# A two-layer attention kernel: residual sums through an identity product, and the seam between the layers cut into pairs of tiles

## The chip, the cores and the metric

The kernel runs on one core of a Trainium2 chip. The core has a matrix engine (TensorE, PE in the profile), a vector engine (VectorE, DVE), a scalar engine (ScalarE, ACT), a general engine (GpSimd, POOL) and SyncE (SP), which here only issues DMAs. The metric is the device time of one execution in microseconds (us); the three timed runs gave 1856.75, 1857.15 and 1862.86, median 1857.15.

## What is computed

Two layers work on x, two sequences (b = 0, 1) of 1024 rows by 512. Cut to the places that matter here:

```
xn = layernorm(x)
x  = x + attention0(xn) + mix(xn)          # layer 0
xn = layernorm(x)
x  = x + attention1(xn) + lora_ffn(xn)     # layer 1, causal, 32 heads, 8 groups

attention0: one head of 128;  out @ Wo + bo
mix:        H_res = (1-g)*I + g*sinkhorn(logits)      # 4x4 per row, 50 iterations
            x_mixed[i] = sum_j H_res[i,j] * xn_stream[j]      # 4 streams of 128
            + a small branch product, spread over the 4 streams
attention1: latent = xn @ Wdown;  k, v = latent @ Wup;  q = xn @ Wq;  out @ Wo
```

## The kernel before

**Tiles and data.** A tile is 128 rows of x; each sequence has eight, t = 0 to 7. `acc[b, t]` (128x512, f32) holds the running residual of a tile through both layers. Every product that must have f32 accuracy is taken in f16: both factors are split into a high and a low part, and three of the four partial products are summed in PSUM (`mm3`, line 83, whose matmul is line 88). There are eight PSUM banks, in three rings: `pp` (four), `s` (three, taken by `srow()`), and `av` (one, `out_tile()`).

**Order.** The program is written out straight, and the scheduler of the language keeps each engine's queue near the written order, filling in instructions that are ready. An engine then runs its own queue in order. Where the order must not be left to the scheduler, the source pins it with `after(...)` or `behind(...)`.

**Layer 0.** For each sequence `front0` normalises and transposes and makes Q, K, V and the logits of the mix. `attn0_rows` (line 457) computes softmax rows, four row blocks per half. `attn0_out` (line 468) multiplies with V, evacuates, splits (lines 476 to 479), and for each of four tiles adds in one PSUM bank the bias (line 484) and the three products with Wo (line 486). VectorE then adds the bank to `acc` (line 488). It is called four times, 16 tiles in all.

**The Sinkhorn chain.** For b = 0 it runs on VectorE (`chain_dve`, line 561): 49 iterations of six small instructions each (lines 576 to 583), every one needing the one before it. It is a generator; `adv(n)` in the main program takes n half iterations of it between other pieces of layer 0, and `adv(200)` (line 997) takes what is left once the attention of b = 1 is written. Line 592 makes the last product, line 527 scales it into `Hm`, and line 529, four times, adds the diagonal. The kernels of the chain lie in one `s` bank.

**The seam.** Layer 1 begins with b = 0. Lines 1011 to 1022 mix, normalise and transpose its tiles in two groups of four (`LG`). Tiles in `MP` (1, 3, 6, 7) are mixed by ScalarE (16 multiplications of 128x128, line 633) and GpSimd (four sums, line 634), the others by VectorE (16 instructions, line 642) from a PSUM copy of `acc` that ScalarE makes (line 614), in an `s` bank for tiles 0 and 2 and in a `pp` bank for tiles 4 and 5. `layernorm_tiles` (line 214) takes the statistics of a group (lines 219, 220), and a short reciprocal square root between VectorE and ScalarE (lines 221 to 224, 201, 202). `normed_T` (line 227) scales (lines 233, 237), splits (238, 240) and issues a transposing DMA per tile (line 242) into `xT`. `after` holds VectorE's j > 0 mixing of group 1 behind group 0's norm (line 224) and ScalarE's j > 1 mixing behind group 0's last split.

**Layer 1's first products.** `start` (line 1024) makes four latent blocks from tiles 0 to 3, the four query blocks of half 0 from the same tiles, four latent blocks from tiles 4 to 7, and then the first keys and values. Each block is 12 matmuls of 512 columns. A latent block is evacuated by four ScalarE and four VectorE instructions of 64x256 (`lat_evac`, line 663). After that the attention of layer 1 goes on to the end of the kernel.

## Time and profile before

| stage of the profiled execution (us from its start) | what happens |
|---|---|
| 0 to 180.5 | layer 0, its Sinkhorn chain interleaved |
| 180.5 to 197.5 | rest of the chain on VectorE, last products of layer 0 |
| 197.5 to 225.2 | mix, norm and transposition of tiles 0 to 3; no matmul |
| 225.2 to 259.7 | layer 1's first products; tiles 4 to 7 follow |
| 261.9 to 1853.7 | attention of layer 1 |

The profiled execution took 1855.46 us, its span from first to last instruction is 1853.7 us, so 1.8 us lie around the span. PE is busy for 93% of the span, DVE 78%, ACT 64%, POOL 49%. In the lines that follow further down, a timeline row reads: start, duration (of one or of a merged run), engine, line, operation, output<-input, shapes, count, and in brackets the idle time before it with what ended that idle time. A row of windows gives, for one stretch, its length and the busy time and count of PE, PEld (weight loads), DVE, ACT and POOL, then the granted TensorE clock, the DMA share and GB/s. A row of waits gives who waited for whom, the sum in us, how often, and the longest.

### The profile page before, as it was taken

To read this page: it belongs to the slowest core of one execution; us is meant where nothing else is said; L and a number is where in the kernel's file an instruction comes from. 1 tells how busy PE (TensorE), PEld (TensorE's weight loads), DVE (VectorE), ACT (ScalarE), POOL (GpSimd) and SP (SyncE) were. 2 spreads that over 40 slices of the span, in tenths; PEclk is the share of its full clock that TensorE was granted. 3 is DMA by queue.
4 is the path that set the end of the run, shared out by engine and by line. 5 is a ranking of instruction groups with operands and counts; after the bars stand their busy time and mean duration, and the time that the engine had idled before them with its cause. 6 is when DMAs were issued, how large, how long until landed. Compare 5 with 4: busy or idle time off the path is not lost. (4 is left out here: it accounts for less than half of the span.)

```text
span 1853.7 us, 35094 instructions
## 1 busy us (share of the span) xinstructions
PE 1715.7 (93%) x11458; PEld 1046.0 (56%) x11458; DVE 1447.6 (78%) x4050; ACT 1194.1 (64%) x2917; POOL 910.6 (49%) x1540
## 2 busy tenths in 40 slices
PE   4756399999999999998999999999999999999998
PEld 3434146566666556655555556666666666656565
DVE  8888978988888877777976867777777777777675
ACT  3848665656676778776544756666666767676554
POOL 5567639768775455647634333424242433335200
PEclk9878699999999999999999999999999999999999
DMA  7435225666574657468546555656565656566455
GB/s 211 82 56 124 67 51 131 143 115 144 113 147 102 143 115 158 111 131 158 137 92 141 130 120 126 146 111 150 107 151 115 142 117 140 117 141 139 101 123 120
DMA packets 707306, 230.26 MB, mean 124 GB/s; under 512 B 689953, under 2 KB 690081, under 8 KB 707122
## 3 DMA queue, kind: packets, MB, share of 16 engines
q1 hardware_dynamic: 691666, 180.75, 47.2%
q0 software_dynamic: 13152, 43.07, 8.5%
q10 hardware_dynamic: 2304, 4.20, 0.7%
q8 instruction: 90, 1.47, 0.4%
q14 instruction: 94, 0.77, 0.1%
HBM read 52.81 MB, written 4.19 MB: 31 GB/s over the span
## 5 line engine op out<-in xcount | busy, mean ns | idle before, releaser
L291 ACT ACTIVATE P<-P,nm 128x1024 f32<-128x1024 f32 (+31 forms) x528 | 391.3, 742 | 250.0 <-DVE nm L283 234.8
L314 DVE SCALAR_TENSOR_TENSOR Phl<-P,r,Phl 128x1024 f16<-128x1024 f32 (+31 forms) x515 | 434.4, 853 | 85.9 <-ACT Phl L308 79.5
L88 PE MATMUL s<-K,Q 128*128 128x512 f16 (+22 forms) x2400 | 440.7, 317 | 19.5 <-DVE P L287 11.6
L345 PE MATMUL av<-PT,V 128*128 128x256 f16 x3648 | 447.7, 274 | 7.5 <-DMA PT<-Phl 6.8
L345 PEld LDWEIGHTS <-V 128*128 128x128 f16 x3648 | 357.0, 98 | 94.7 <-DMA PT<-Phl 8.3
L308 ACT ACTIVATE Phl<-P,r 128x1024 f16<-128x1024 f32 (+31 forms) x515 | 370.0, 731 | 22.3 <-DMA PT<-Phl 3.3
L88 PE MATMUL pp<-xT,wq 128*128 128x512 f16 x1536 | 372.9, 381 | 6.3 <-DVE acc L737 3.2
L88 PE MATMUL pp<-wo,ao 128*128 128x512 f16 x1536 | 369.9, 379 | 2.9 <-ACT ao L104 2.7
L94 POOL TENSOR_SCALAR f2k<-f2k 128x512 f32<-128x512 f32 x164 | 109.5, 668 | 499.9 <-DVE Phl L314 444.5
L88 PEld LDWEIGHTS <-Q 128*128 128x128 f16 x2400 | 223.2, 98 | 178.2 <-issue 28.4
L88 PEld LDWEIGHTS <-wq 128*128 128x128 f16 x1536 | 149.6, 98 | 173.8 <-issue 8.5
L88 PEld LDWEIGHTS <-ao 128*128 128x128 f16 x1536 | 149.4, 98 | 156.5 <-ACT ao L104 4.8
L287 DVE TENSOR_SCALAR_CACHE_REDUCE P<-s 128x512 f32<-128x512 f32 (+15 forms) x272 | 152.6, 562 | 21.7 <-PE s L88 19.7
L283 DVE CUSTOM_DVE_ANT_0 P<-s,mask,nm 128x272 f32<-128x272 f32 (+15 forms) x256 | 157.3, 615 | 8.7 <-PE s L88 1.0
L303 ACT ACTIVATE r<-r 128x1 f32<-128x1 f32 x528 | 96.2, 193 | 66.2 <-DVE r L302 65.4
L319 POOL MEMSET Phl<- 128x192 f16 (+2 forms) x384 | 72.6, 209 | 133.5 <-DMA PT<-Phl 95.7
L302 DVE RECIPROCAL r<-r 128x1 f32<-128x1 f32 x528 | 79.2, 155 | 75.3 <-ACT P L291 72.1
L104 ACT ACTIVATE ao<-av 128x512 f16<-128x512 f32 x128 | 75.1, 587 | 92.2 <-PE av L345 92.0
L283 DVE CUSTOM_DVE_ANT_0 P<-s,mask 128x32 f32<-128x32 f32 (+15 forms) x256 | 104.3, 432 | 27.6 <-PE s L88 27.1
L104 ACT ACTIVATE Q<-pp 128x512 f16<-128x512 f32 x128 | 74.5, 582 | 76.7 <-PE pp L88 72.2
L737 DVE SCALAR_TENSOR_TENSOR acc<-pp,acc 128x512 f32<-128x512 f32 x128 | 87.4, 682 | 41.0 <-PE pp L88 40.6
L105 DVE SCALAR_TENSOR_TENSOR Q<-pp,Q 128x512 f16<-128x512 f32 x128 | 87.6, 684 | 34.9 <-ACT Q L104 34.6
(254 smaller groups left out, 2119.1 us busy)
## 6 DMA issues: line engine op xcount, KB each, us to landing
f2k<-in_Wq POOLq DMA_DIRECT2D x64, 256.0 KB, 3.2
f2k<-in_WoT POOLq DMA_DIRECT2D x64, 256.0 KB, 3.3
PT<-Phl SPq DMA_TRANSPOSE x528, 3.2
acc<-in_x SPq DMA_DIRECT2D x16, 256.0 KB, 4.6
f2k<-in_Wup POOLq DMA_DIRECT2D x16, 256.0 KB, 3.5
out<-acc ACTq DMA_DIRECT2D x16, 256.0 KB, 3.5
xr<-in_x SPq DMA_DIRECT2D x12, 256.0 KB, 4.1
f2k<-in_Wlat POOLq DMA_DIRECT2D x8, 256.0 KB, 5.5
```

What stands on the lines that cost most here:

```text
L88: nc.tensor.matmul(dst, lhs(l), rhs(r), start=(i == 0 and j == 0), stop=(i == n - 1 and j == 2))
L94: first = G.tensor_scalar(stage, stage, scale, 1.0, ALU.mult, ALU.mult)
L104: A.activation(hl_hi, src, AF.Copy, scale=scale)
L105: return V.scalar_tensor_tensor(hl_lo, src, scale, hl_hi, ALU.mult, ALU.subtract)
L283: last_row[0] = V.tensor_tensor_reduce(Pm[:, o:o + w], pt[:, :w], mask[:, 512 - w:], -scale, first, ALU.add, ALU.min, nm[:, k:k + 1])
L287: last_row[0] = V.tensor_scalar(Pm[:, o:o + w], pt[:, :w], -scale, first, ALU.mult, ALU.min, accum_out=nm[:, k:k + 1])
L291: A.activation(Pm[:, :W], Pm[:, :W], AF.Exp, bias=last, scale=-1.0, accum_out=r[:, 0:1])
L303: A.activation(r[:, 1:2], r[:, 1:2], AF.Copy, scale=PSCALE)
L308: A.activation(hl[:, 0, :W], Pm[:, :W], AF.Copy, scale=r[:, 1:2])
L314: lo = V.scalar_tensor_tensor(hl[:, 1, :W], Pm[:, :W], r[:, 1:2], hl[:, 0, :W], ALU.mult, ALU.subtract)
L345: nc.tensor.matmul(p, Vh(j, l), PT(r * nj + j), start=(j == 0 and k == 0), stop=(j == nj - 1 and k == 2))
L737: V.scalar_tensor_tensor(acc[b, t], p, 1.0 / 256.0, acc[b, t], ALU.mult, ALU.add)
```

## The change

1. In `attn0_out` an identity matrix `eye` of f32 (value 1024, made by GpSimd at the start) times `acc` is summed into the PSUM bank by TensorE. ScalarE then writes the bank, scaled by 1/1024, to `acc`. VectorE's sum at line 488 is gone. For b = 1, half 1, three banks are kept; their writes, and the whole fourth product, are put behind the first pair's last split.
2. The last product of the chain writes `Hm` directly in the wanted order, the scaling is in place, and the four diagonal sums become one with a stride of five.
3. The seam goes in four pairs of tiles; `MP` is (1, 3, 5, 7), so each pair has one tile for VectorE and one for ScalarE and GpSimd. The PSUM copies of tiles 0, 2, 4 and 6 all lie in `s` banks. The pinning of the order is by pairs, and there is none between the third and fourth.
4. `start` takes four latent blocks and two query blocks by quarters of 256 columns: first all six for the first pair, then all six for the second. Query blocks 2 and 3 are whole. The latent blocks of tiles 4 to 7 go by quarters again. Keys and values alternate by half.

```diff
-LG = ((0, 1, 2, 3), (4, 5, 6, 7))
-MP = (1, 3, 6, 7)
+LG = ((0, 1), (2, 3), (4, 5), (6, 7))
+MP = (1, 3, 5, 7)
...
+    eye = T("tw", [P, P], bufs=1)
+    G.memset(eye, 1024.0)
+    G.affine_select(eye, eye, [[-1, P]], ALU.is_equal, 0.0, base=0, channel_multiplier=1)
...
+    def proj_quarter(p, w, xT, k):
+        mm3(p[:, 256 * (k % 2):256 * (k % 2) + 256],
+            [(lambda l, c=c: w(c, l), lambda r, c=c: xT[:, 2 * k:2 * k + 2, 2 * c + r, :])
+             for c in range(NC)])
...
             for r in range(2):
                 nc.tensor.matmul(p, row, bo[:, r], start=(r == 0), stop=False)
+            nc.tensor.matmul(p, eye, acc[b, 4 * half + q], start=False, stop=False)
             for k, (l, r) in enumerate(PASSES):
...
-            V.scalar_tensor_tensor(acc[b, t], p, 1.0 / 1024.0, acc[b, t], ALU.mult, ALU.add)
+        def store(q, p):
+            A.activation(acc[b, 4 * half + q], p, AF.Copy, scale=1.0 / 1024.0)
+        if later is None:
+            for q in range(4):
+                store(q, product(q))
+            return
+        ps3 = [product(q) for q in range(3)]
+        later += [lambda q=q: store(q, ps3[q]) for q in range(3)] + [lambda: store(3, product(3))]
...
-        V.tensor_scalar(Hb, M if b else M.rearrange("p t j i -> p t i j"), gs[:, 0:1], None, ALU.mult)
-        for n in range(4):
-            V.tensor_scalar(Hb[:, :, n, n], Hb[:, :, n, n], gs[:, 1:2], None, ALU.add)
+        V.tensor_scalar(Hb, Hb, gs[:, 0:1], None, ALU.mult)
+        diag = Hb.rearrange("p t i j -> p t (i j)")[:, :, 0::5]
+        V.tensor_scalar(diag, diag, gs[:, 1:2], None, ALU.add)
...
-                    got["d"] = srow() if t < 4 else PP()
+                    got["d"] = srow()
...
-                with after(*(last_rs[:1] if pool else last_rs[1:] if j else last_mix)):
+                with after(*(last_rs[:1] if pool else (last_rs[1:] or last_mix) if j else last_mix)):
...
-        last_rs[:] = [last_hi[0], stt]
+        last_rs[:] = [last_hi[0], stt] if k < 2 else []
+        if k == 0:
+            with after(last_hi[0]):
+                for f in sums:
+                    f()
...
-        for mc in range(4):
-            lat_evac(0, mc, 0, lat_block(0, wl[:, mc], 0))
-        for u in range(4):
-            q(u)
-        for mc in range(4):
-            lat_evac(0, mc, 1, lat_block(0, wl[:, mc], 1))
-        for f in kvf:
-            f()
+        def quarters(todo, th):
+            for k in range(2):
+                for w, p, evacuate in todo:
+                    proj_quarter(p, w, xT1[0], 2 * th + k)
+                    if k:
+                        evacuate(p)
+        quarters(lats(0) + [q_first(u, srow()) for u in range(2)], 0)
+        q(2)
+        q(3)
+        quarters(lats(1), 1)
+        for k in (0, 2, 1, 3):
+            kvf[k]()
```

`lats(th)` puts three latent blocks in `pp` banks and the fourth in the `av` bank; `q_first` evacuates a query block from an `s` bank as `qproj` did.

More of the change, by code (lines that the diff above doesn't have):

```diff
@@ L466, in attn0_rows, with attn0_out @@
         return PTs
-    def attn0_out(b, half, Vh, PTs):
+    def attn0_out(b, half, Vh, PTs, later=None):
         p = out_tile()
@@ L479, in attn0_out, with product @@
         G.tensor_tensor(hl[:, 1], ao, hl[:, 0], ALU.subtract)
-        for q in range(4):
-            t = 4 * half + q
+        def product(q):
             p = PP()
@@ L487, in attn0_out @@
                                  start=False, stop=(k == 2))
-            V.scalar_tensor_tensor(acc[b, t], p, 1.0 / 1024.0, acc[b, t], ALU.mult, ALU.add)
+            return p
+        def store(q, p):
[6 more added lines that the diff above has]
+        later += [lambda q=q: store(q, ps3[q]) for q in range(3)] + [lambda: store(3, product(3))]
     def sinkhorn(b, lg):
@@ L558, in chain_pool @@
                 x = Kt
-        V.tensor_tensor(M, M, over_i(bb), ALU.mult)
+        V.tensor_tensor(Hm[b], M, over_i(bb), ALU.mult)
     def chain_dve(b, Z, M, aa, bb, over_i, over_j, f2):
@@ L591, in chain_dve @@
             yield
-        V.tensor_tensor(f2(M), f2(M), over_j(bb), ALU.mult)
+        V.tensor_tensor(Hm[b].rearrange("p t i j -> p t j i"), M, bc(bb, 3, 4), ALU.mult)
     xr_more, last_mix, last_stt, last_rs = {}, [], [None], []
@@ L728, in qproj, with q_evac @@
     def qproj(b, w, Q, hh, half):
-        p = proj_T(lambda c, l: w[:, l, c, :], xT1[b], half)
+        q_evac(Q, hh, proj_T(lambda c, l: w[:, l, c, :], xT1[b], half))
+    def q_evac(Q, hh, p):
         evac(p.rearrange("p (b q) -> p b q", q=QR), Q[:, 0, :, hh, :], Q[:, 1, :, hh, :], 0.125)
@@ L799, in layer1_attn, with q_first @@
         kvs[0], fs = kv0
-        start(fs[2:], lambda u: q_unit(0, u))
+        def q_first(u, p):
+            if u == 0:
+                Qs[0, 0] = T("Q", [P, 2, NS // 2, 4, QR], F16, bufs=2)
+            return lambda c, l: qw[0, u][:, l, c, :], p, lambda p: q_evac(Qs[0, 0], u, p)
+        start(fs[2:], q_first, lambda u: q_unit(0, u))
         for hh in range(4):
@@ L995, in tile_model @@
         PTs = attn0_rows(1, half, *f0[1][:2], lambda: adv(CD))
-        attn0_out(1, half, f0[1][2], PTs)
+        sums = []
+        attn0_out(1, half, f0[1][2], PTs, sums if half else None)
     adv(200)
@@ L1021, in tile_model, with start, lats @@
             xT_tile(0, t, NP[t])
-        last_rs[:] = [last_hi[0], stt]
-    def start(kvf, q):
-        latents(0)
-        for mc in range(4):
-            lat_evac(0, mc, 0, lat_block(0, wl[:, mc], 0))
-        for u in range(4):
-            q(u)
-        for mc in range(4):
-            lat_evac(0, mc, 1, lat_block(0, wl[:, mc], 1))
-        for f in kvf:
-            f()
+        last_rs[:] = [last_hi[0], stt] if k < 2 else []
[3 more added lines that the diff above has]
+                    f()
+    def start(kvf, q_first, q):
+        latents(0)
+        lat = lambda mc: lambda c, l: wl[:, mc, l, c, :]
+        def lats(th):
+            return [(lat(mc), out_tile() if mc == 3 else PP(), lambda p, mc=mc: lat_evac(0, mc, th, p))
+                    for mc in range(4)]
+        def quarters(todo, th):
[10 more added lines that the diff above has]
+            kvf[k]()
     gw1 = gating_w()
```

## The prediction

> **What bounds the kernel now.** I first asked for busy time by stretches of the span, with the borders set where the seam between the layers begins and ends (the columns are explained above).
>
> ```profile
> 180.50:197.50 17.00, 12.34 (x77) 6.96 (x76) 14.46 (x45) 6.04 (x10) 9.08 (x11) 0.99 0.51 141
> 197.50:225.20 27.70, 0.02 (x1) 0.05 (x2) 26.85 (x88) 22.20 (x71) 20.89 (x18) 0.51 0.22 42
> 225.20:244.30 19.10, 17.51 (x73) 7.32 (x74) 15.30 (x37) 10.67 (x25) 16.18 (x23) 0.91 0.49 112
> 244.30:261.80 17.50, 16.87 (x79) 7.55 (x77) 7.97 (x17) 7.67 (x18) 0.00 (x0) 1.00 0.07 27
> ```
>
> From 197.5 to 225.2 no matmul runs, and VectorE is busy for 26.85 of 27.70 us: there DVE is the bound. From 225.2 on PE is the bound, and stays so: the same view by larger stretches has PE busy for 300.00 of 300 us twice between 1100 and 1700. So what arrives earlier at PE's first product of layer 1, and isn't lost again before the first scores, comes off the end one for one. Next I read the waits of PE, and the timelines of PE (first fence) and DVE (second).
>
> ```profile
> PE pp L88 <- DMA xT<-wo: 29.6, 1, 29.6
> ...
> 225.18 9.57 PE L88 MATMUL pp<-xT,PT 128*128 128x512 f16 x36 [29.63 <-DMA xT<-wo]
> 236.34 2.76 PE L88 MATMUL pp<-xT,PT 128*128 128x512 f16 x12 [1.59 <-DVE cmp L105]
> 238.98 10.53 PE L88 MATMUL pp<-xT,wq 128*128 128x512 f16 x48
> 249.35 10.52 PE L88 MATMUL pp<-xT,PT 128*128 128x512 f16 x48
> 259.71 1.46 PE L88 MATMUL pp<-cmp,wo 128*128 128x512 f16 x6
> 261.86 0.31 PE L88 MATMUL s<-K,Q 128*128 128x32 f16 x4 [0.69 <-ACT K L104]
> ```
>
> PE waits once, 29.6 us, for the transposes of tiles 0 to 3. Then it works with one gap of 1.59 us to the first keys at 259.71. Tiles 4 to 7 don't hold it: their last transpose is issued at about 241, lands 3.2 us later, and the blocks that read it start at 249.35.
>
> ```profile
> 192.46 0.29 DVE L581 TENSOR_TENSOR sk<-s,sk 128x128 f32<-128x128 f32 x1
> 193.46 0.69 DVE L488 SCALAR_TENSOR_TENSOR acc<-pp,acc 128x512 f32<-128x512 f32 x1 [0.71 <-PE pp L486]
> 194.07 0.28 DVE L582 TENSOR_REDUCE sk<-sk 128x32 f32<-128x128 f32 x1
> 194.26 1.28 DVE L488 SCALAR_TENSOR_TENSOR acc<-pp,acc 128x512 f32<-128x512 f32 x2
> 195.46 0.34 DVE L583 RECIPROCAL sk<-sk 128x32 f32<-128x32 f32 x1
> 195.72 0.63 DVE L488 SCALAR_TENSOR_TENSOR acc<-pp,acc 128x512 f32<-128x512 f32 x1
> 196.26 0.28 DVE L592 TENSOR_TENSOR sk<-sk,sk 128x128 f32<-128x128 f32 x1
> 196.57 0.33 DVE L527 TENSOR_SCALAR Hm<-sk,gs 128x128 f32<-128x128 f32 x1
> 196.94 0.64 DVE L529 TENSOR_SCALAR Hm<-Hm,gs 128x8 f32<-128x8 f32 x4
> 197.48 6.29 DVE L642 SCALAR_TENSOR_TENSOR s<-xr,Hm,s 128x128 f32<-128x128 f32 x24
> ```
>
> The end of the Sinkhorn chain is a bare sequence on DVE, and line 488 stands in its way: its sums are queued between the chain's steps, and one waits 0.71 us for PE with the chain behind it.
>
> **Part 1, the sum leaves DVE.** After the last softmax row (180.5) eight sums of line 488 lie in the chain, four from 185.53 to 188.33 and four from 193.46 to 196.26. By start times, from each to the chain's next instruction, they hold DVE for 1.21 + 0.60 + 0.54 + 0.61 + 1.20 + 0.54 = 4.7 us, and two waits for PE of 0.96 and 0.71 us go with them: 6.4 us off. The eight sums of b = 0 (90.9 to 106.1) I cost at nothing: the chain follows its written places (91 of its about 100 steps are placed before the last `adv`), and DVE then idles 2.74 us at 117.6 for a product of b = 1, whose path goes through POOL, busy without a break from 100.8 to 124.4. If the chain did use that time, up to 4.7 + 1.3 = 6 us more would go.
>
> In place of each sum come a ScalarE write and an f32 matmul. The write's nearest row is the copy at line 614 (0.58 to 0.60 us, 128x512 between PSUM and SBUF). ACT is busy for only 6.04 of 17.00 us around 190 and has idle stretches of 11.4 and 10.2 us near 90 and 105; without that cover 16 writes would cost 9.6 us. No f32 matmul is in this trace. Below, it is one f16 matmul, 0.216 us (48 starts in 10.37 us). Above, it is all four partial products of two split factors on a cold array: six f16 matmuls at 85.6 took 2.74, so 4 x 0.46 = 1.83 us. I take 0.8 us, the nearest row: the three-pass product at line 486 (0.82). The Trainium skill, "FP8 and Floating Point Precision", section "TensorE Precision Notes", says that true f32 takes four passes through the array; that would be an estimated 0.86 us and change nothing below. Cover: before each group PE idles for ACT's split (4.96, 0.91, 3.84 and 0.60 us) with `acc` and `eye` ready, so the identity products of the first three tiles go there; the fourth, waiting for a bank, adds 0.8 us. POOL reaches the sums that need them at 108 to 113, after line 488 was done at 106.1, so 0.8 us is hidden. Uncovered, all 16 would be 13 us, at worst 29. The last group's fourth product runs in PE's idle stretch. `eye` is two POOL instructions at about 2 us (rows there: 0.52 for 128x512, 0.24 for a 32x32 selection); if the selection grows with its rows and columns it is 4 us at most, beside POOL's 3.57 us wait for the first weights, so nothing to 1 us.
>
> **Part 2, the chain's end.** Four diagonal sums (0.54 us from first start to the next instruction) become one (0.2): 0.3 us off; the strided product may give 0.1 back. Together with part 1 the mix starts at 197.5 - 6.4 - 0.3 = 190.8, call it E.
>
> **Part 3, pairs.** DVE's tile costs 16 instructions at 0.262 (24 in 6.29) = 4.2 us. ACT's tile is 16 at 0.295 (32 in 9.45) = 4.7, and POOL's last sum 1.3 after it. ACT also has lines 476 and 478 (1.3 us) near 190. So tile 1 is mixed at E + 7.5 where four tiles took until 208.9. Statistics and the short chain: 0.7 + 0.2 + 0.2, 0.6 on ACT with its hand-overs, six DVE instructions 1.5 (229.09 to 230.56): E + 11. Scaling 0.8, two splits 0.6 each, two remainders 0.65 each, overlapped: the second transpose is issued at about E + 14, and with 3.2 us to landing and its 1.25 us of issue PE can start at E + 18 = 209. Before, it was 197.5 + 27.7. The last writes (1.8 us of ACT) follow.
>
> Each further pair repeats this, but with its j = 0, 1 products done while the norm of the pair before runs. What is queued behind the new waits: on DVE 12 mix instructions (3.1), two remainders (1.3) and a scaling (0.5); then POOL's last sum, statistics 0.7, norm 2.5, scaling and splits 2.5, transposes 4.5. I count 10 to 11 us per pair: landings at E + 18, 29, 39. The fourth competes with evacuations of the first latent blocks (16 x 0.42 = 6.7 us of DVE) and lands at about E + 47. DVE's whole work up to there (mix 17, statistics 7, norms 6, scaling and remainders 6.5, evacuations 8) is 44.5 us, which agrees.
>
> **Part 4, quarters.** A matmul of 256 columns takes 0.109 us (24 of line 345 in 2.78 with a last drain of 0.16), so halves cost 12 x (2 x 0.109 - 0.216) = 0.02 us a block more: nothing. Sequence: pair 1, six quarters, 72 x 0.109 = 7.9 and a cold start of 1.7, E + 18 to 27.6; wait to 29; pair 2, 7.9, to 37; query blocks 2 and 3, 5.2, to 42; pair 3, 5.2, to 47.5; pair 4, 5.2, to 52.7 or, with the hand-over, 53. First keys at E + 53 = 244 where they were at 259.7. Gain 15.7 us. The keys' order adds nothing: they need only latent blocks 0 and 1. The `s` banks can bite: query block 1 needs the bank of tile 4, free at about E + 26, when PE gets there at E + 26; a stall of some 1 us is likely. I take 15 us.
>
> The trace on restarts: from 225.2 to 228.6 PE did 9 matmuls at a granted clock of 0.51, then 18 in the next 3.4 us at 1.00, so a cold start costs 1.7 us. The Trainium skill, "TensorE: Matmul & The Clock Gate", section "Part 1: The HAM clock gate", says the array falls back to half rate after an idle window of about 3.4 us. That speaks against work in bursts: by it each gap of that length between pairs would cost a further 1.7, an estimated 5 us for three; with the gaps counted above, none.
>
> **The sum.** 1855.46 - 15 = 1840.5 on the profiled execution, which lies 1.7 us under the median, so 1842.2 against 1857.15. Its own range: 6 us more from b = 0 and a few from earlier landings, 1832; 6 us less from pairs that come late, 1848.
>
> **Rivals.** *The last pair is late.* If nothing of a norm is hidden, a pair takes 12.5 us: landings at E + 18, 30.5, 43, 55.5, keys at E + 60.7, a gain of 8: 1849. For it: DVE is full already (26.85 of 27.70). Against: the work is the same and the last landing before was 46.8 after the chain's end. *The chain doesn't end earlier*, because the scheduler puts something else in the freed places or the f32 products hold b = 1 back: E stays at 197.5, pairs alone give 15 - 6.7 = 8: 1849. *Slower*: the f32 products are long and lie on PE in front of layer 0's products with V. At 1.83 us and all exposed, 29 us against a gain of 15: 1871. It decides from 25 us, that is 1.55 us on each of 16. For it: the clock is 0.64 to 0.93 in those stretches. Against: PE idles 3.8 and 5.0 us in front of two of the groups.
>
> **Chances.** Forecast 0.62; last pair late 0.15; chain not earlier 0.10; slower 0.13. 0.5%, about what a measurement tells from no change, is 9.3 us: faster means under 1847.9. The forecast and a few of the middle cases give 0.65; within 0.5%, 0.21; slower 0.14. The range takes in the middle cases: 1832 to 1853.
>
> **What would show it.** In the profile after: no DVE sum in the chain, the first mix instruction at about 191; first matmul of layer 1 near 209, first keys near 244, with gaps between the quarters under 2 us; the f32 products near 0.8 us in PE's old idle stretches. Wrong if the mix starts at 197 or later, if PE waits more than 5 us in sum between the quarters, if layer 0's products with V move back, or if the attention of layer 1 loses what the seam gained.

## The result, and the profile after

The change is slower: 1874.51 us median of four runs (1871.76 to 1875.19) against 1857.12 for the kernel before (1856.75 to 1862.86), ratio 1.0084 [1.0065, 1.0103]. The forecast was 1842.2, with a range of 1832 to 1853. The profiled execution took 1874.25 us, with a span of 1872.5.

Busy time by stretches of the kernel after, with the columns of the first fence of the prediction. It starts at the same time, 180.5, and the other borders lie at the same events (start of the mix, first product, the middle of the products, first scores):

```profile
180.50:195.50 15.00, 11.02 (x25) 3.41 (x24) 10.92 (x33) 7.40 (x14) 11.64 (x12) 0.61 1.01 240
195.50:221.90 26.40, 16.74 (x67) 7.38 (x66) 12.45 (x37) 14.51 (x37) 6.57 (x6) 0.69 0.18 41
221.90:256.00 34.10, 23.67 (x163) 17.20 (x163) 31.92 (x91) 24.58 (x72) 24.50 (x27) 0.85 0.27 64
256.00:276.60 20.60, 16.03 (x133) 12.12 (x132) 11.84 (x30) 10.02 (x25) 6.29 (x10) 0.95 0.22 52
```

In the second row DVE, full before (26.85 of 27.70), is busy for 12.45 of 26.40 us: it waits. And from the first product to the first scores PE is busy for 39.70 of 54.70 us, where it was 34.38 of 36.60. PE's timeline shows the gaps:

```profile
221.93 3.83 PE L88 MATMUL pp<-xT,PT 128*128 128x256 f16 x24
...
237.21 6.02 PE L88 MATMUL pp<-xT,PT 128*128 128x256 f16 x36 [6.21 <-DMA xT<-wo]
...
248.82 2.76 PE L88 MATMUL pp<-xT,wq 128*128 128x512 f16 x12 [1.66 <-DVE cmp L105]
254.14 4.45 PE L88 MATMUL pp<-xT,wq 128*128 128x512 f16 x12 [2.56 <-DVE cmp L105]
...
266.87 4.10 PE L88 MATMUL pp<-xT,PT 128*128 128x256 f16 x36 [3.03 <-DMA xT<-wo]
...
273.60 0.38 PE L88 MATMUL pp<-cmp,wo 128*128 128x512 f16 x1 [1.32 <-ACT cmp L104]
...
276.61 0.32 PE L88 MATMUL s<-K,Q 128*128 128x32 f16 x4
```

The first product comes 3.3 us earlier than before (221.93 against 225.18), the first keys 13.9 later (273.60 against 259.71). Two gaps of PE wait for transposes, two for evacuations of the latent blocks (`cmp`). The second kind was in the prediction's own fence already: `236.34 ... [1.59 <-DVE cmp L105]`, the fourth latent block waiting for the first one's evacuation. I read it as a small stall; it is the sign that the blocks run out of banks. Here the section on the kernel is wrong: line 46 gives the ring `s` four banks and `pp` three, not the other way round.

DVE's timeline of the kernel after, at the end of the chain and behind the first mix:

```profile
186.56 1.77 DVE L323 SCALAR_TENSOR_TENSOR Phl<-P,r,Phl 128x1024 f16<-128x1024 f32 x1 [2.80 <-ACT Phl L317]
...
195.18 0.26 DVE L550 TENSOR_SCALAR Hm<-Hm,gs 128x32 f32<-128x32 f32 x1
195.48 4.66 DVE L663 SCALAR_TENSOR_TENSOR s<-xr,Hm,s 128x128 f32<-128x128 f32 x12
...
212.35 0.69 DVE L222 BATCH_NORM_STATS2 bnst<-acc 128x6 f32<-128x512 f32 x1 [10.11 <-POOL acc L655]
```

The sums are gone from the chain, but it waits 2.80 us for the last softmax row (L323), and the mix starts at 195.48, only 2.0 us earlier. DVE then stands for 10.11 us until tile 1 is mixed. ACT's timeline says why, for both:

```profile
176.19 0.67 ACT L486 ACTIVATE f2k<-av,bqkv 128x512 f32<-128x512 f32 x1
...
180.73 1.14 ACT L300 ACTIVATE P<-P,nm 128x1024 f32<-128x1024 f32 x1
...
193.73 0.60 ACT L635 ACTIVATE s<-acc 128x512 f32<-128x512 f32 x1 [1.74 <-DVE sk L602]
195.49 1.65 ACT L632 ACTIVATE P<-P,rsa 128x512 f32<-128x512 f32 x2 [1.16 <-DMA P<-in_x]
204.11 0.69 ACT L486 ACTIVATE f2k<-av,bqkv 128x512 f32<-128x512 f32 x1 [6.97 <-PE av L354]
204.69 3.60 ACT L654 ACTIVATE f2k<-xr,Hm 128x128 f32<-128x128 f32 x12
```

The last row's exponential (L300) stands 4.54 us behind the evacuation of the first half's product with V (L486). The multiplications of tile 1 (L654) stand in ACT's queue behind the evacuation of the last product with V (L486), and that waits 6.97 us for PE. In the kernel before ACT had that evacuation (L476) done long before the mix, and the last softmax row ended earlier (ACT's timeline, then DVE's):

```profile
174.54 0.67 ACT L476 ACTIVATE f2k<-av,bqkv 128x512 f32<-128x512 f32 x1
175.11 1.14 ACT L291 ACTIVATE P<-P,nm 128x1024 f32<-128x1024 f32 x1
...
190.34 0.69 ACT L476 ACTIVATE f2k<-av,bqkv 128x512 f32<-128x512 f32 x1
```

```profile
179.11 1.46 DVE L314 SCALAR_TENSOR_TENSOR Phl<-P,r,Phl 128x1024 f16<-128x1024 f32 x1 [0.32 <-ACT Phl L308]
```

So two things make the product late. The last row ends at 188.3 instead of 180.6. And from there to the evacuation it takes 15.8 us instead of 9.8; four f32 products lie in front of it on PE from 188 on, 1.87 + 1.87 + 1.05 + 0.97 = 5.8 us:

```profile
187.06 1.01 PE L493 MATMUL pp<-wo,row 1*128 1x512 f16 x2 [3.51 <-ACT acc L502]
187.99 2.07 PE L495 MATMUL pp<-acc,tw 128*128 128x512 f32 x2
189.86 1.49 PE L497 MATMUL pp<-wo,wo 128*128 128x512 f16 x3
...
198.68 1.12 PE L495 MATMUL pp<-acc,tw 128*128 128x512 f32 x2
199.73 0.60 PE L493 MATMUL pp<-wo,row 1*128 1x512 f16 x2
```

### The profile page after: what moved, and what is told of

Its sections match the earlier page's. It is cut to its first block, busy times and chain, and to the rows that moved or that the text cites. A ratio compares the mean times of both kernels' runs of the same rounds, so it can differ in the third digit from the quotient of the medians.

```text
span 1872.5 us, 35422 instructions
## 1 busy us (share of the span) xinstructions
PE 1742.9 (93%) x11610; PEld 1065.6 (57%) x11610; DVE 1447.5 (77%) x4042; ACT 1203.3 (64%) x2937; POOL 909.9 (49%) x1542
## 4 chain that ended last, share of the span: by engine, by line
PE 46%; DVE 2%; DMA 1%; issue 1%; POOL 1%; ACT 1%; SPq 0%; ACTq 0%; POOLq 0%; DVEq 0%
PE pp L88 25%; PE av L354 11%; PE s L88 10%; DMA PT<-Phl 1%; DVE Phl L323 0%; DVE P L296 0%; DVE f2k L914 0%; ACT Phl L317 0%; DMA twT<-twhl 0%; DMA f2k<-in_Wq 0%; POOL wo L243 0%; DVE P L292 0%; DMA xT<-wo 0%; POOL f2k L94 0%; DVE Q L105 0%
## 5 line engine op out<-in xcount | busy, mean ns | idle before, releaser
L300 ACT ACTIVATE P<-P,nm 128x1024 f32<-128x1024 f32 (+31 forms) x528 | 391.3, 742 | 261.4 <-DVE nm L292 247.4
L323 DVE SCALAR_TENSOR_TENSOR Phl<-P,r,Phl 128x1024 f16<-128x1024 f32 (+31 forms) x515 | 433.3, 852 | 95.8 <-ACT Phl L317 89.0
L88 PE MATMUL pp<-xT,wq 128*128 128x512 f16 x1512 | 368.9, 382 | 9.6 <-DVE cmp L105 4.2
L88 PEld LDWEIGHTS <-Q 128*128 128x128 f16 x2400 | 222.7, 98 | 169.1 <-issue 17.9
L311 DVE RECIPROCAL r<-r 128x1 f32<-128x1 f32 x528 | 78.5, 155 | 75.3 <-ACT P L300 72.2
L96 POOL TENSOR_TENSOR wo<-f2k,wo 128x512 f16<-128x512 f32 x84 | 109.0, 1299 | 3.8
```

What stands on the lines that cost most here:

```text
L88: nc.tensor.matmul(dst, lhs(l), rhs(r), start=(i == 0 and j == 0), stop=(i == n - 1 and j == 2))
L96: G.tensor_tensor(hl_lo, stage, hl_hi, ALU.subtract)
L300: A.activation(Pm[:, :W], Pm[:, :W], AF.Exp, bias=last, scale=-1.0, accum_out=r[:, 0:1])
L323: lo = V.scalar_tensor_tensor(hl[:, 1, :W], Pm[:, :W], r[:, 1:2], hl[:, 0, :W], ALU.mult, ALU.subtract)
```

## The experiments

**Theory A**: the identity half (parts 1 and 2) is the loss, through products on PE and writes on ScalarE; the seam gains. **Theory B**: the seam half (parts 3 and 4) is the loss, through the late reload of x; the identity half is harmless. Neither held alone, and the later runs look for the cause in each half. Ratios are against runs of the kernel before taken alongside (its medians there are 1858.2 to 1860.0 for the experiments), with 95% intervals. E is the start of DVE's mix; all four landmarks are from the profiled execution of the kernel named, in us.

| kernel | median | ratio | profiled | E | first product | first keys | E to keys |
|---|---|---|---|---|---|---|---|
| before | 1857.12 | 1 | 1855.46 | 197.5 | 225.2 | 259.7 | 62.2 |
| after | 1874.51 | 1.0084 [1.0065, 1.0103] | 1874.25 | 195.5 | 221.9 | 273.6 | 78.1 |
| e1 parts 1+2 | 1871.38 | 1.0076 [1.0046, 1.0105] | 1866.44 | 195.8 | 233.7 | 268.1 | 72.3 |
| e2 parts 2+3+4 | 1868.05 | 1.0051 [1.0033, 1.0069] | 1868.16 | 198.1 | 214.2 | 265.8 | 67.7 |
| e3 e2, x ahead | 1874.31 | 1.0078 [1.0059, 1.0097] | 1874.26 | 199.8 | 217.4 | 266.9 | 67.1 |
| e4 after, x ahead | 1873.06 | 1.0075 [1.0056, 1.0095] | 1870.69 | 195.9 | 220.5 | 270.0 | 74.1 |
| e5 after, output late | 1865.93 | 1.0035 [1.0017, 1.0052] | 1865.02 | 193.9 | 211.7 | 264.2 | 70.3 |
| e6 pairs only | 1867.71 | 1.0046 [1.0028, 1.0064] | 1868.42 | 199.2 | 229.0 | 267.8 | 68.6 |
| e7 quarters only | 1858.44 | 0.9999 [0.9983, 1.0016] | 1856.35 | 196.0 | 220.4 | 255.4 | 59.4 |
| e8 before, output late | 1866.72 | 1.0040 [1.0022, 1.0059] | 1858.92 | 194.9 | 223.6 | 266.3 | 71.4 |
| e9 e5, identity b = 1 | 1869.66 | 1.0047 [1.0030, 1.0063] | 1861.76 | 194.3 | 210.8 | 263.4 | 69.1 |
| e10 e6 repaired | 1866.76 | 1.0034 [1.0021, 1.0047] | 1865.74 | 200.4 | 228.1 | 268.6 | 68.2 |
| e11 e2 repaired | 1870.69 | 1.0052 [1.0036, 1.0068] | 1871.04 | 199.4 | 217.0 | 268.6 | 69.2 |
| e12 all repaired | 1872.17 | 1.0055 [1.0040, 1.0070] | 1868.16 | 194.9 | 211.5 | 268.0 | 73.1 |
| e13 e11, s banks | 1868.74 | 1.0062 [1.0043, 1.0081] | 1868.48 | 197.9 | 215.5 | 262.4 | 64.5 |
| e14 e1, no residual | 1861.18 | 1.0005 [0.9992, 1.0019] | 1862.98 | 197.6 | 229.4 | 264.5 | 66.9 |
| e15 identity b = 1 | 1866.92 | 1.0038 [1.0023, 1.0052] | 1868.19 | 197.1 | 228.3 | 267.3 | 70.2 |
| e16 e15, order | 1862.96 | 1.0023 [1.0011, 1.0034] | 1861.41 | 192.0 | 222.3 | 263.3 | 71.3 |
| e17 e16, more order | 1866.29 | 1.0039 [1.0023, 1.0055] | 1865.73 | 194.1 | 222.4 | 267.3 | 73.2 |
| e18 e17, DVE sums | 1860.53 | 1.0007 [0.9993, 1.0020] | 1862.91 | 195.0 | 222.4 | 262.6 | 67.6 |

Single runs of one kernel lie up to 13.7 us apart, so differences of a few us are read from the intervals; the profiled execution of e1, e8, e9 and e12 is its fastest, 4 to 8 us under the median.

### The two halves: e1 to e4

**e1**, on the kernel before:

```diff
+            nc.tensor.matmul(p, eye, acc[b, t], start=False, stop=False)
...
-            V.scalar_tensor_tensor(acc[b, t], p, 1.0 / 1024.0, acc[b, t], ALU.mult, ALU.add)
+            A.activation(acc[b, t], p, AF.Copy, scale=1.0 / 1024.0)
```

with the short end of the chain as in the change.

> Before with parts 1 and 2 of the change alone (identity product, ScalarE write at once, shorter end of the chain), the seam still in two groups of four. Theory A, the identity products in layer 0 are the loss: the softmax rows of b = 1 half 1 end some 7 us later than before, the evacuation of the last V product stands in ScalarE's queue ahead of the mix and waits for TensorE, layer 1's first product starts at 230 or later (225.2 before), and the time is 1863 to 1870. Theory B, the seam is the loss and the identity products are harmless: the mix starts near 191, the first product near 219, the time is 1849 to 1852.

Measured 1871.38, with the first product at 233.7, much as theory A has it. **e2** is the change with VectorE's sum and without `eye`; the short end of the chain stays:

```diff
-            nc.tensor.matmul(p, eye, acc[b, 4 * half + q], start=False, stop=False)
...
-            A.activation(acc[b, 4 * half + q], p, AF.Copy, scale=1.0 / 1024.0)
+            V.scalar_tensor_tensor(acc[b, 4 * half + q], p, 1.0 / 1024.0, acc[b, 4 * half + q], ALU.mult, ALU.add)
...
-        attn0_out(1, half, f0[1][2], PTs, sums if half else None)
+        attn0_out(1, half, f0[1][2], PTs, None)
```

> The change with VectorE's sum put back in place of the identity product and nothing deferred; pairs, quarters and the shorter chain end stay. Theory A: the seam alone gains, first keys at about 252 (259.7 before), 1847 to 1852. Theory B, in pairs x of tiles 2 and 3 is reloaded only when tiles 0 and 1 give their xr slots back, and all later pairs slip: first keys at 265 or later, 1862 to 1870.

Measured 1868.05, with the first keys at 265.8, as theory B has it: both halves are slower by themselves. **e3** is e2, and **e4** the whole change, with the loads taken out of the pairs:

```diff
+    every = [mix0_units(0, t, f0[0][5], t in MP) for t in range(NT)]
+    for t in range(4):
+        every[t][0]()
     for k, ts in enumerate(LG):
-        units = [mix0_units(0, t, f0[0][5], t in MP) for t in ts]
+        units = [every[t][t < 4:] for t in ts]
```

> e2 with the four loads of x (tiles 0 to 3) issued ahead of the pairs, so that they get the four xr slots before the first pair's norm takes two. Theory A: a few us under e2, 1843 to 1849. Theory B: 8 us or more under e2, as the slots are the loss.

> The whole change with the four loads of x issued ahead of the pairs. Theory A: pair 1 need not wait for its x, so some 5 to 8 us come back, 1866 to 1870, but the first product still starts near 222 and the time stays above before. Theory B: nearly all of the loss comes back, 1857 or less.

Measured 1874.31 and 1873.06. In e3 the second pair's first transpose follows the first's by 10.2 us (e2: 13.9), so the reload did cost 3.7 us; but the third comes 24.7 us later, behind the evacuations, and the time is no better. Theory B falls as a whole, and what it named is real.

### The seam: e6, e7, e10, e11, e13

**e6** is e2 with the old `start`, whole blocks in the old order; **e7** the kernel before with the new `start`, `LG` in fours:

```diff
-        quarters(lats(0) + [q_first(u, srow()) for u in range(2)], 0)
-        q(2)
-        q(3)
-        quarters(lats(1), 1)
-        for k in (0, 2, 1, 3):
-            kvf[k]()
+        for mc in range(4):
+            lat_evac(0, mc, 0, lat_block(0, wl[:, mc], 0))
+        for u in range(4):
+            q(u)
+        for mc in range(4):
+            lat_evac(0, mc, 1, lat_block(0, wl[:, mc], 1))
+        for f in kvf:
+            f()
```

(e6; in e7 the same lines the other way round.)

> Pairs of tiles with the old sums on VectorE and the old order of layer 1's first products: whole blocks of 512 columns, four latent blocks, four query blocks, four latent blocks. Theory E (evacuations in the way): the pairs are slow because the first products, which start 11 us earlier, are evacuated by VectorE and ScalarE in front of the norms of pairs 3 and 4; without the quarters PE starts when pair 2 has landed, at about 227, the norms of pairs 3 and 4 run first, first scores at 262 to 264, time 1857 to 1861. Theory N (pairs cost by themselves): four norms with their hand-overs instead of two and the x slots taken by the scaled tiles make the last pair late whatever PE does; first scores at 267 to 270, time 1866 to 1870.

> Groups of four tiles and VectorE's sums as before, only the new order of layer 1's first products: quarters of 256 columns, two query blocks in the s banks, a latent block in the av bank, keys and values alternating. Nothing can start before the four tiles have landed, so by itself it should gain nothing. Theory E and theory N both: first product at 225, first scores within 2 us of 262, time 1855 to 1860. Theory B (banks and order): blocks held open over six quarters keep the banks of pp, s and av longer, and the query blocks 2 and 3 and the keys in another order cost by themselves; first scores at 264 to 267, or the same scores and 4 to 6 us lost in the first rows of layer 1's attention, time 1861 to 1866.

Measured 1867.71 and 1858.44. The quarters cost nothing that can be measured; the pairs lose by themselves (theory N). SyncE's and ScalarE's timelines of e6 show x of tiles 2 and 3 loaded only when tiles 1 and 0 are mixed, and its scaling and mixing behind that:

```profile
203.74 1.61 SPq L625 DMA_DIRECT2D xr<-in_x  x2
```

```profile
210.32 1.50 ACT L627 ACTIVATE xr<-xr,rsa 128x512 f32<-128x512 f32 x2
211.91 4.78 ACT L649 ACTIVATE f2k<-xr,Hm 128x128 f32<-128x128 f32 x16
```

ACT had ended tile 1 at 203.7. **e10** repairs e6, **e11** repairs e2: x ahead as in e3, `last_rs` set after every pair, and (last two lines) in e11 also a pin on the evacuations:

```diff
-        last_rs[:] = [last_hi[0], stt] if k < 2 else []
+        last_rs[:] = [last_hi[0], stt]
...
-                    if k:
-                        evacuate(p)
+                    if k:
+                        with after(*(last_rs if th == 0 else [])):
+                            evacuate(p)
```

> Pairs with VectorE's sums and whole blocks (as e6), with two repairs: x of tiles 0 to 3 is loaded ahead, and the last pair's mixing too is held behind the norm of the pair before. Theory X (slots and order): of e6's 8 us, about 4 come from pair 2, whose x is loaded only when a slot of tile 0 or 1 is free, and 4 from the norm of pair 3, whose small steps lie among the mixing of pair 4; then transposes at 211, 221, 231 and the last at 246 to 249 (the first latent evacuations still stand in front of the fourth norm), first scores at 263 to 266, time 1859 to 1863. Rival F (four norms cost what they cost): first scores at 268 to 271, time 1865 to 1869.

> Pairs and quarters with VectorE's sums (as e2), with three repairs: x of tiles 0 to 3 ahead, the last pair's mixing behind the norm before it, and the evacuations of the first six blocks behind the fourth norm, so that VectorE and ScalarE do all norms before any evacuation. Theory X (slots and order): the last transpose is issued at 238 to 242 (e2: 255.1), first keys at 253 to 257, first scores at 256 to 260; time 1852 to 1857, but up to 4 us of that may be lost again in the first rows of layer 1's attention, as in e7. Rival K (banks): PE then stands still for want of a free bank while six blocks wait for their evacuation, and first scores come at 262 to 266, time 1858 to 1863.

Measured 1866.76 and 1870.69: e10 as rival F says, e11 slower than either theory. In e11 the first transposes of the pairs are issued at E + 13.1, 23.3, 33.3 and 43.9, a pair every 10 us as forecast, and still it is slow. PE's timeline of e11:

```profile
217.02 5.50 PE L88 MATMUL pp<-xT,PT 128*128 128x256 f16 x36 [19.36 <-DVE bnst L219]
...
227.13 4.10 PE L88 MATMUL pp<-xT,PT 128*128 128x256 f16 x36 [0.69 <-DMA xT<-wo]
...
232.38 2.78 PE L88 MATMUL s<-xT,wq 128*128 128x256 f16 x24
249.21 7.73 PE L88 MATMUL pp<-xT,wq 128*128 128x512 f16 x24 [14.04 <-DVE cmp L105]
...
268.60 0.38 PE L88 MATMUL pp<-cmp,wo 128*128 128x512 f16 x1 [1.17 <-ACT cmp L104]
```

From 235.2 to 249.2 PE waits for a `pp` bank: three latent blocks hold all three until DVE, busy for 39.52 of the 43.80 us from E to 243.2, has ended the norms and evacuates them; the pin keeps the evacuations behind the fourth norm. **e13** puts query blocks 2 and 3 into `s` banks, so that PE needs no fourth `pp` bank there:

```diff
-        q(2)
-        q(3)
+        for u in (2, 3):
+            w, p, evacuate = q_first(u, srow())
+            for k in range(2):
+                proj_quarter(p, w, xT1[0], k)
+            with after(*last_rs):
+                evacuate(p)
```

> e11 with one thing more: query blocks 2 and 3 too lie in s banks and are taken while the latent blocks wait, so that PE needs no fourth pp bank (the pp ring has three banks, all held by the first latent blocks). Theory K (banks alone): PE's stall of 14 us in e11 goes, first keys come at 254 to 257, time 1853 to 1858. Theory V (VectorE's work is the bound): of the 14 us only the 8 us come back that blocks 2 and 3 took behind it; the second latent blocks still wait until VectorE has evacuated the first ones, behind four norms, at about 249, so first keys at 259 to 262, level with before's 259.7, and after the usual loss in the first rows the time is 1860 to 1865.

Measured 1868.74; first keys at 262.4, at the edge of what theory V said (259 to 262), but the time is worse than it said. Its stretches, and those of the kernel before from the same event (DVE's evacuations of the first latent blocks nearly done):

```profile
197.90:248.90 51.00, 22.46 (x193) 19.36 (x193) 46.62 (x138) 34.86 (x104) 34.88 (x36) 0.73 0.30 64
248.90:262.40 13.50, 12.34 (x96) 10.22 (x97) 4.92 (x13) 4.18 (x12) 1.60 (x4) 0.87 0.12 40
```

```profile
197.50:243.60 46.10, 16.83 (x70) 7.05 (x71) 42.15 (x124) 32.86 (x96) 37.00 (x40) 0.67 0.32 71
243.60:259.70 16.10, 16.10 (x76) 7.28 (x75) 6.48 (x14) 5.95 (x14) 0.08 (x1) 1.00 0.12 34
```

In both DVE is busy for 91% of the first stretch (42.15 of 46.10, 46.62 of 51.00). Of the 4.5 us more in e13 some 2 us are the evacuations of three query blocks (three times 0.69), which come behind the border in the kernel before; from E to the first keys DVE is busy for 51.54 us against 48.63, 2.9 more. In this order, with the pin, the second latent blocks wait until DVE is through and start at E + 51.0, no earlier to speak of than before (249.35, E + 51.9). Of the orders tried with pairs and VectorE's sums e10 is the fastest (1.0034), and it is still slower than the kernel before.

### The identity half: e5, e8, e9, e14, e15, e16

**e5** is the change with the whole last output step, not only its writes, behind the first pair's last split; **e8** the kernel before with the short end of the chain and the same move (sums on VectorE, groups of four):

```diff
+        if half:
+            sums.append(lambda: attn0_out(1, 1, f0[1][2], PTs))
+        else:
+            attn0_out(1, 0, f0[1][2], PTs)
```

> The whole change, with one thing moved: the last output step of layer 0 (b = 1, half 1: product with V, its evacuation and split on ScalarE, the four products with Wo, the writes) is written behind the first pair's last split, where the change puts only the writes. Theory H (head of the line): most of what the identity half loses is that the evacuation of the last product with V stands in ScalarE's queue in front of the mix of tile 1 and waits there 7 us for PE; then tile 1's mix starts within 2 us of tile 0's, the first product of layer 1 comes at 212 to 215 (after: 221.9), and the time falls by 6 to 9 us to 1865 to 1868. Theory Q (queue order of the later pairs): the last pair's landing decides, and it is set by VectorE's and ScalarE's work between pairs, so an earlier first product is given back: time within 3 us of 1874.

> The kernel before with the short end of the chain and with the last output step of layer 0 (b = 1, half 1, VectorE's sums kept) written behind the first group's last split, so that its four sums and their wait for PE leave the chain; no identity product, groups of four, old order of products. If a shorter chain is worth what it saves (four sums of 0.6, a wait of 0.71, 0.3 us of the diagonal: about 3.5 us), the mix starts at 194 and the time is 1852 to 1855. If the time in the seam is set elsewhere (ScalarE's and GpSimd's share of the mix, or VectorE's whole backlog, to which the four sums return behind the split), the time is 1856 to 1860.

Measured 1865.93 and 1866.72. In e5 the mix of tile 1 starts at 194.5 (after: 204.7), the first product at 211.7, and the time falls by 8.6 us, within the 6 to 9 that theory H named: the place of the last output step, in ScalarE's queue and in PE's, is about half of the change's loss. In e8 the same move does harm: the late products wait for their split, which stands in ScalarE's queue behind 12 multiplications of the second group (L478 at 216.53). DVE waits 6.88 us for these products, the copies of tiles 4 and 5, which need the `pp` banks that the products hold, come only at 222.90, and the second group's first transpose at 246.1 instead of 233.9.

**e9** is e5 with the identity product for b = 1 only:

```diff
-            nc.tensor.matmul(p, eye, acc[b, 4 * half + q], start=False, stop=False)
+            if b:
+                nc.tensor.matmul(p, eye, acc[b, 4 * half + q], start=False, stop=False)
...
-            A.activation(acc[b, 4 * half + q], p, AF.Copy, scale=1.0 / 1024.0)
+            if b:
+                A.activation(acc[b, 4 * half + q], p, AF.Copy, scale=1.0 / 1024.0)
+            else:
+                V.scalar_tensor_tensor(acc[b, 4 * half + q], p, 1.0 / 1024.0, acc[b, 4 * half + q], ALU.mult, ALU.add)
```

> The change with the last output step behind the first pair (as in the run e5), and with the identity product for the second sequence only: the eight sums of the first sequence are VectorE's again. Theory L (a chain step in ScalarE's queue): with the identity product everywhere, the Sinkhorn chain runs ahead in the stretch at 115 us, and the logarithm of its 25th iteration then stands in ScalarE's queue between the scalings of the second sequence's tiles and waits 2.8 us for VectorE; that puts the first softmax row of b = 1 at 148 to 150 instead of 146.3. Then here the first row of b = 1 is at 146 to 147, the mix starts at 190.5 to 192 (e5: 193.9; the prediction said 190.8), and the time is 2 to 4 us under e5: 1862 to 1864. Rival P (the f32 products themselves): the lateness comes from the products on PE in the second sequence's rows; mix at 193 to 195 and the time within 1 us of e5.

Measured 1869.66. The first softmax row of b = 1 starts at 142.8 (e1 149.7, after 148.3, before 146.3): the first sequence's half does push the rows back. But the mix starts at 194.3 all the same, as rival P has it, and the time fits neither side of that expectation. ACT's and DVE's timelines of e9:

```profile
174.88 0.69 ACT L486 ACTIVATE f2k<-av,bqkv 128x512 f32<-128x512 f32 x1 [5.05 <-PE av L354]
...
179.44 1.13 ACT L300 ACTIVATE P<-P,nm 128x1024 f32<-128x1024 f32 x1
```

```profile
175.83 0.35 DVE L608 RECIPROCAL sk<-sk 128x32 f32<-128x32 f32 x1
180.70 0.16 DVE L311 RECIPROCAL r<-r 128x1 f32<-128x1 f32 x1 [4.51 <-ACT P L300]
180.78 0.27 DVE L601 TENSOR_TENSOR sk<-s,sk 128x128 f32<-128x128 f32 x1
```

The last row's exponential (L300) stands in ACT's queue behind the evacuation of the first half's product with V, and the row's reciprocal (L311) in DVE's queue in front of the chain. So the chain stands still for 4.51 us. It is no f32 product that this evacuation waits for: PE's product with V itself waits 4.10 us for the transposes of a softmax row. In the kernel before the same evacuation is at 174.54, 0.57 us ahead of that exponential; in the kernel after, 4.54 us ahead, there without a wait of its own, but with five other instructions in between.

**e14** is e1 without the identity product, so that acc gets the output product alone:

```diff
-            nc.tensor.matmul(p, eye, acc[b, t], start=False, stop=False)
```

> e1 (parts 1 and 2 alone) without the identity product: ScalarE still writes the bank to acc, but the residual is left out of it, so acc gets the output product alone and the kernel computes something else. Theory P (the f32 products on PE are the loss): the 11 us of e1 go, time 1852 to 1859. Theory O (the writes on ScalarE and the order that the scheduler makes of ScalarE's queue are the loss; the products lie in PE's idle time): time 1866 to 1872, as e1, first product of layer 1 at 230 to 234.

Measured 1861.18, ratio 1.0005 against e1's 1.0076: nearest to theory P, 2 us above its range. The f32 products, or the order and the reading of `acc` that come with them, are the identity half's loss; ScalarE's writes by themselves are not. The last product with V is evacuated at 197.6 in e14, 202.2 in e1, 190.3 before.

**e15** is the kernel before with the short end of the chain and the identity product for b = 1 only; **e16** adds one order: the first half's output, from its evacuation on, is written behind the exponential of the last row. `attn0_out` becomes a generator that yields in front of the evacuation of its product with V:

```diff
+        def between():
+            adv(CD)
+            rows_done[0] += 1
+            if half and rows_done[0] == 4:
+                run(first)
+        PTs = attn0_rows(1, half, *f0[1][:2], between)
+        part = attn0_out(1, half, f0[1][2], PTs)
+        if half:
+            run(part)
+        else:
+            next(part)
+            first = part
```

> The kernel before with the short end of the chain and the identity product for the second sequence only, at the written place (no late output), groups of four, old order of products. If the first sequence's half of the products made the rows late: mix at 190 to 192, first product 219 to 223, time 1850 to 1856. If the loss sits at the end of the second sequence, where the evacuation of the product with V stands ahead of the last softmax row and of the mix in ScalarE's queue: mix at 193 to 196, first product 228 to 234, time 1862 to 1870.

> e15 with one order changed: the evacuation of the first half's product with V, and what follows from it, is written behind the last softmax row's exponential, so that the row does not wait behind it in ScalarE's queue. In e9 the chain lost 4.5 us at that place. If that wait is where the chain's freed time went: mix at 189 to 191, the prediction's E, and if ScalarE reaches the mix of tile 1 by 195, first product at 217 to 222 and time 1849 to 1855. If the evacuation of the last product with V then blocks ScalarE in front of the mix instead: mix of tile 1 at 197 to 203, first product 225 to 232, time 1858 to 1867.

Measured 1866.92 and 1862.96. In e15 DVE waits 7.67 us for the last exponential, in e16 0.3, and E is 192.0: within 1.2 us of the forecast's 190.8. The chain's gain is there once one queue is in order. It is then lost behind E: four of ScalarE's writes lie between its multiplications, the first norm waits 2.50 us for ScalarE, PE waits 2.80 and 2.39 us for evacuations and runs cold behind the second; first keys at 263.3. PE's timeline of e16 has:

```profile
235.76 2.76 PE L88 MATMUL pp<-xT,PT 128*128 128x512 f16 x12 [2.80 <-DVE cmp L105]
240.92 12.22 PE L88 MATMUL pp<-xT,wq 128*128 128x512 f16 x48 [2.39 <-DVE cmp L105]
```

### Together: e12, e17, e18

**e12** is e11 with e9's identity and late output step. **e17** is e16 with the last writes behind the first group's split, the PSUM copies in `s` banks and the first latent evacuations behind the second norm. **e18** is e17 with VectorE's sums, as in e2 (`store` on VectorE, no `eye`).

(`later` and `sums` are the change's own.)

```diff
-        part = attn0_out(1, half, f0[1][2], PTs)
+        part = attn0_out(1, half, f0[1][2], PTs, sums if half else None)
...
+            with after(last_hi[0]):
+                for f in sums:
+                    f()
...
-                    got["d"] = srow() if t < 4 else PP()
+                    got["d"] = srow()
...
-            lat_evac(0, mc, 0, lat_block(0, wl[:, mc], 0))
+            p = lat_block(0, wl[:, mc], 0)
+            with after(last_rs[1]):
+                lat_evac(0, mc, 0, p)
```

> All repairs together: the identity product for the second sequence only, the last output step behind the first pair, x ahead, the last pair's mixing held, the first evacuations behind the fourth norm. If the repairs add (mix 4 to 6 us earlier than in e11): last transpose at 235 to 239, first scores at 252 to 256, time 1848 to 1853. If the late output step takes the same places in ScalarE's and GpSimd's queues as the pairs (as in e8, where it cost the second group 12 us): first scores within 2 us of e11's or later, time at or above e11's.

> Groups of four, old order of layer 1's products, short end of the chain, identity product for the second sequence only, and three places in the queues mended: the first half's output behind the last softmax row (as e16), ScalarE's last four writes behind the first group's last split, and the first latent evacuations behind the second group's norm; PSUM copies in s banks. Theory Q (the gain was there, and was lost in the order of ScalarE's and VectorE's queues): mix at 191 to 193 as in e16, first product at 218 to 221 (before 225.2), first keys at 254 to 257 (before 259.7), time 1850 to 1856, the first version under before. Theory V (VectorE and ScalarE together bound the seam whatever the order): first keys at 258 to 262, time 1857 to 1863.

> The same as e17 with VectorE's sums instead of the identity product and ScalarE's writes: what the identity product itself is worth when the queues are in order. By the prediction's first part the mix should start 5 to 6 us later than in e17 (197 to 199), and the first keys and the time should follow by as much. If ScalarE's writes and the f32 products cost elsewhere what VectorE saves, the time is within 2 us of e17's.

Measured 1872.17, 1866.29, 1860.53. The repairs don't add, and no version is faster than the kernel before. PE's waits of e17, from 205 to 330:

```profile
PE pp L487 <- ACT acc L497: 17.6, 1, 17.6
PE pp L88 <- DVE cmp L105: 9.4, 1, 9.4
PE pp L88 <- ACT acc L497: 1.9, 1, 1.9
```

The evacuations that I put behind the norm make PE wait 9.4 us for a bank (4.6 in e18, with the same pin): a pin that helps one queue empties another. Neither theory Q nor theory V has keys as late as 267.3. e18 against e17 says that in this order the identity product costs 0.3% (1.0007 [0.9993, 1.0020] against 1.0039 [1.0023, 1.0055]) instead of bringing 5 us; its expectation missed.

### What is lost behind the first scores

The lag of layer 1's n-th softmax row (ScalarE's exponential) behind the same row of the kernel before, in us:

| row | 0 | 12 | 24 | 128 | 256 | end |
|---|---|---|---|---|---|---|
| after | 15.1 | 9.7 | 17.1 | 17.5 | 18.7 | 18.9 |
| e2 | 6.5 | -2.5 | 6.9 | 9.8 | 12.4 | 12.7 |
| e6 | 8.0 | 8.0 | 8.0 | 9.0 | 13.3 | 12.9 |
| e7 | -2.9 | -8.2 | -0.8 | -0.2 | 0.3 | 0.9 |
| e13 | 4.1 | -1.4 | 9.5 | 8.8 | 12.3 | 13.0 |

With the new `start` the rows run ahead up to row 12 and fall back by row 24. In e7 2.9 us at the first row become nothing, in e2 and e13 more is lost than was won. PE's waits of e7 from 262 to 330, against 0.7 us for its longest before:

```profile
PE pp L88 <- DVE acc L745: 3.3, 1, 3.3
```

So first keys and first scores are no safe measure of the end either. Between rows 208 and 256 another 2 to 5 us go in some kernels (after 3.2, e2 2.3, e6 2.9, e13 5.0; e7 none). The mix of b = 1 is over by then (824.7 us in the kernel before, where row 208 starts at 867.3); its tiles are transposed and its latent blocks made there. That was not followed up.

## Why the prediction was wrong

**Part 1, the sum leaves DVE.** Its size was nearly right, its place wrong. In e16 E is 192.0 (forecast 190.8): from the end of the last softmax row to the mix it is 12.6 us instead of 16.9, with one half iteration of the chain (1.03 us) more in it, so 5.4 us of the forecast's 6.7; the rest of the earlier E is a row that ends 1.2 us earlier. The step that failed: "ACT is busy for only 6.04 of 17.00 us around 190", taken as cover. A busy share doesn't say who stands behind whom. In the change the last row's exponential stands in ScalarE's queue 4.54 us behind the evacuation of a product with V (0.57 before), and the mix of tile 1 behind another, which waits 6.97 us for PE. That the first sequence's eight sums could be moved at no cost failed too: the first row of b = 1 starts at 147.2 to 149.7 in the four kernels that have the first sequence's products, at 141.2 to 146.3 in the others. Of the 2.0 us in the change alone little could be said, since e7, which is the kernel before up to there, has this row 2.0 us earlier than the kernel before (144.3 against 146.3).

**The f32 product.** I took 0.8 us, within 0.216 and 1.83. From its start to the next instruction it is 0.97 to 1.05 us warm and 1.87 cold, each as two records. The Trainium skill, "FP8 and Floating Point Precision", section "TensorE Precision Notes", counts four passes, by which I had an estimated 0.86; measured it is 13 to 22% longer warm, and twice that cold, and two of the last group's four run cold. That "before each group PE idles for ACT's split" held for three products of the group before the last (154.3 to 158.8). Its fourth product and three of the last group's stand in PE's queue ahead of the last product with V.

**Part 2.** From the chain's last product to the mix 1.04 us, before 1.22: 0.2 us, near the 0.3 (in e16 it is 1.62).

**Part 3, pairs.** 10 to 11 us per pair is what e11 and e13 show (10.2, 10.0, 10.6), with x ahead and the norms pinned. In the change it was 15.4, 19.1 and 10.6. The first product at E + 18 was right where the output step isn't in the way (E + 16.0 in e2, 17.9 in e5, 17.6 in e11 and e13); in the change it is E + 26.4. The step that failed named what is queued on DVE behind the waits, but not the x slots that the scaled tiles take, nor that nothing holds the last pairs' norms in front of the evacuations.

**Part 4, quarters.** The cost of halves was right: 12 matmuls of 256 columns start 1.31 us apart, 0.109 each, and e7 loses nothing. The sequence (pair 1, pair 2, query blocks 2 and 3, pair 3, pair 4) failed: I counted PE's blocks and the landings, and not the banks. The blocks of pairs 3 and 4 need `pp` banks that are free only when DVE, busy with the norms, has done its share of the evacuations. DVE's whole work of 44.5 us, "which agrees", was the bound itself (46.62 measured in e13): the second latent blocks start behind it, at E + 51, and 13.5 us lie from there to the keys. That is E + 64.5, not E + 53, and no better than the 62.2 of the kernel before.

**The clock.** After the gap of 6.21 us above, 36 matmuls took 6.02 us where the same blocks warm took 4.10; after one of 2.56 us, twelve took 4.45 instead of 2.76, at a granted clock of 0.60. The Trainium skill, "TensorE: Matmul & The Clock Gate", section "Part 1: The HAM clock gate", has a cold array after an idle window of about 3.4 us. The rule spoke against the change; my count of gaps made it zero, and it was two restarts of 1.9 and 1.7 us. The shorter gap also went cold, which by that window alone needn't happen, and length alone doesn't decide it here: after the change's gap of 3.03 us and e16's of 2.80 us the clock was 1.00, after e16's of 2.39 us 0.58.

**The rivals.** The slower one (f32 products, 1871) came nearest. That they lie on PE in front of layer 0's products with V was right, and e14 shows that the loss of parts 1 and 2 comes with them, in their own time or in the order that the scheduler makes; its price was not: they are not 29 us long, and 5.8 us of them stand in front of the last product. That the time came out near 1871 is luck. "The last pair is late" had the right direction and too small a size: its landings E + 18, 30.5, 43, 55.5 stand against transposes issued at E + 22, 37, 56 and 67. Two of my signs for failure came: gaps of PE between the quarters, 13.5 us in sum, and layer 0's last product with V, evacuated 13.8 us later.

**Open.** Why the order that comes with the products costs 0.7% in e1 and 0.3% in e17 was seen in single waits, not shown as a sum. Why e13 isn't faster than e11, whose keys are 6.2 us later, is open, and so is the loss between rows 208 and 256.

## What to carry to other kernels

An engine that is 35% busy is no cover: follow the freed time through the in-order queue of every engine that the chain crosses, and look for an instruction there that waits for someone else. A pipeline that is cut finer starts earlier and ends when its bound engine has done all its work; first sum that engine's work up to the last thing needed, and count the buffers that stay held until then. A short wait for an evacuation in the old profile, here 1.59 us, can tell of a ring that is just long enough.

## What the runs showed of the hardware

A 128x512 f32 matmul against a 128x128 identity shows as two records; it costs 4.5 to 4.9 f16 matmuls warm (0.97 to 1.05 against 0.216 us) and 1.87 us cold. A gap of PE of 2.56 us, after one of 1.66 and 2.76 us of work, brought the granted clock down (0.60) as one of 6.21 us did (0.50), and so did one of 2.39 us (0.58); after gaps of 2.80 and 3.03 us it was 1.00. Matmuls of 256 columns cost half of 512, to the hundredth of a us.
